# A graph network layer: node loads cut into rows of 2048 bytes and issued in one go, the first weight loads moved to GpSimd's queue

## The chip, the core and the metric

The kernel runs on one core of a Trainium2 chip. The metric is the device time of one execution in microseconds; the time of a kernel is the median of its runs. Five engines work side by side, each with its own queue of instructions: TensorE (PE in the profile; PEld is its weight load), VectorE (DVE), ScalarE (ACT), GpSimd (POOL) and SyncE (SP), which here only issues DMAs. DMAs are issued by SP, ACT and GpSimd; all of them are carried out by the same 16 DMA engines.

## What is computed

There are 12500 nodes with 160 features (64 scalars `s`, 32 vectors `v` of 3 components) and 400000 edges, sorted by destination.

```
h_s = s @ lin1_ws * a / sqrt(64)          # a: one number per node
h_v = v @ lin1_wv * a / sqrt(32)          # on the 32 channels, for each component
w   = silu(edge_attr_64 @ fc_w1 / 8) @ fc_w2 / 8        # 224 numbers per edge
es, ev = h_s[src], h_v[src]
messages per edge: w1*es*e0, w4*(ev . e1)/sqrt(3), (w2*es) e1, w3*ev*e0, w5*(ev x e1)/sqrt(2)
agg = sum of the messages over the edges of each destination / 4
o   = agg @ lin2, scaled by a; pre = x @ sc, scaled by a, + o
y   = silu of 64 scalars, sigmoid gates times the vectors
out = layernorm(x + y) over the 160 features
```

## The kernel before

**Three stages.** A first stage lays a table `h_tab` of `h_s` and `h_v` (12500 rows of 640 bytes) into device memory. The second stage walks over the 3125 tiles of 128 edges, in steps of four tiles: GpSimd gathers the table rows of each tile by its `src` indices (`gather`, L463, the indirect DMA of L467), TensorE makes the edge weights, VectorE the products, TensorE sums them into windows of 16 nodes, which are then mapped and added to the accumulator. The third stage, most of which lies inside the second, finishes blocks of nodes. A gather needs the whole table, so the second stage begins when the last row of `h_tab` has landed. A loop at the end, taken only for unusual destinations, does not run here.

**The first stage** (L226 to L360) works in six chunks of 2048 nodes (`CH`) and a last one of 212. For each chunk `load` issues three loads on SP: `xa` rows 0 to 63 (the scalars of x, transposed, L242), `xa` rows 64 to 127 (two components of the vectors, L243) and `xz` (the third component, in four quarters of 512 nodes, over 128 partitions, L248; L251 for the last chunk). TensorE multiplies 128 nodes at a time with `l1` (a block-diagonal matrix of lin1_ws and twice lin1_wv; L327) and with `l1z` (four times lin1_wv; L343); VectorE multiplies by the node attribute `at` into `ht` (L330, L346); GpSimd stores `ht` into `h_tab` (L357). Of `ht` there are three buffers, so chunk 3 reuses that of chunk 0 once its store has landed. Before chunk 3, `bases()` (L299) takes the first destination of each block of tiles from the first row of `dt` and spreads it over the partitions as `lo`. The last 84 rows of the table are stored by SP (L360).

**The order around the change.** All engines work in the order of the program text here (`manual_schedule`). SP issues the loads of chunk 0 first; ACT issues the loads of `at`, `l1` (three) and `l1z` (four), scales `l1` and `l1z` by 1/sqrt(64) or 1/sqrt(32) (L287) and issues the load of the first row of `dt` (L289). The node loads of the other chunks follow on SP, then the first indices and edge attributes (`ahead`, L152 and L153) and the edge network's weights (L296, L297). GpSimd makes the identity and three iotas before its first store. After the table GpSimd also issues the first edge features (`load_chunk(0, nc.gpsimd)`, L202) and the whole `dt` (L364), and then gathers for the rest of the kernel. The framework gives the DMAs of SP and ACT eight completion semaphores in rotation, those of GpSimd another eight; a DMA waits until the one that had its semaphore before has landed.

Of the kernel before, what the change touches and what calls it, by code (L numbers as in the profile page):

```python
# [10 lines left out]
F32 = mybir.dt.float32  # L11
# [9 lines left out]
P = 128  # L21
S = 64
V = 32
# [7 lines left out]
W = 16  # L31
Q = 4
KB = 4
# [20 lines left out]
def gnn_kernel(  # L54
# [21 lines left out]
    nc = tc.nc  # L76
    N = x.shape[0]
    NT = attr.shape[1]
# [4 lines left out]
    NB = -(-TT // BT)  # L83
    RATE = round(N / NB)
    assert NP >= N - 1 + W

    consts = ctx.enter_context(tc.tile_pool(name="consts", bufs=1))
# [71 lines left out]
    def index(t):  # L159
        a0, idx, _ = ahead(t)  # L160
        return idx[:, t - a0:t - a0 + 1]
# [32 lines left out]
    def load_chunk(c, queue=nc.sync, mark=None):  # L194
# [4 lines left out]
        for half, n in enumerate(halves):  # L199
# [4 lines left out]


    ident = consts.tile([P, P], F32, name="ident")
    make_identity(nc, ident)
    iota_i = consts.tile([P, W], I32, name="iota_i")
    nc.gpsimd.iota(iota_i, pattern=[[1, W]], base=0, channel_multiplier=0)
    eps = consts.tile([P, 1], F32, name="eps")  # L210
    nc.vector.memset(eps, 1e-5)

    w1 = consts.tile([2 * S, 2 * S], F32, name="w1")
    nc.vector.memset(w1, 0.0)

    w2 = consts.tile([2 * S, 2, NWT], F32, name="w2")
    nc.vector.memset(w2, 0.0)
    l2 = consts.tile([P, 11, V3], F32, name="l2")
    nc.vector.memset(l2, 0.0)
    share = ends_pool.tile([1, NB], I32, name="share")  # L220
    even = NB // (2 * KB) * 2 * KB
    nc.gpsimd.iota(share[:, :even], pattern=[[2 * KB * RATE, even // (2 * KB)], [RATE, KB], [KB * RATE, 2]],
                   base=0, channel_multiplier=0)
    nc.gpsimd.iota(share[:, even:], pattern=[[RATE, NB - even]], base=even * RATE, channel_multiplier=0)

    U = 4  # L226
    dt = ends_pool.tile([P, TT], I32, name="dt")
    lo = ends_pool.tile([P, NB], F32, name="lo")
    CH = 4 * U * P
    starts = list(range(0, N, CH))  # L230
    with tc.tile_pool(name="nodes", bufs=len(starts)) as nodes, tc.tile_pool(
        name="nodes_ps", bufs=6, space=PSUM
# [3 lines left out]
        def load(c0):  # L236

            cn = min(CH, N - c0)
            quarters = 4 if cn == CH else 1
            assert quarters == 4 or cn <= U * P  # L240
            xa = nodes.tile([P, CH], F32, name="xa")
            nc.sync.dma_start(xa[:S, :cn], xs_t[:, c0:c0 + cn])  # L242
            nc.sync.dma_start(xa[S:, :cn], xv_t[:2 * V, c0:c0 + cn])  # L243
            xz = nodes.tile([P, U * P], F32, name="xz")
            cq = cn // quarters
            z = xv_t[2 * V:, c0:c0 + cq]
            if quarters == 4:
                nc.sync.dma_start(xz[:, :cq], bass.AP(tensor=z.tensor, offset=z.offset,  # L248
                                                      ap=[[z.ap[0][0], V], [cq, 4], [1, cq]]))
            else:  # L250
                nc.sync.dma_start(xz[S:S + V, :cq], z)  # L251
            loaded.append((c0, cn, quarters, cq, xa, xz))

        load(starts[0])
        at = consts.tile([P, NT], F32, name="at")
        nc.scalar.dma_start(at, attr)

        l1 = consts.tile([P, P], F32, name="l1")
        nc.vector.memset(l1, 0.0)
        nc.scalar.dma_start(l1[:S, :S], lin1_ws)  # L260
        for i in range(2):
            r = slice(S + i * V, S + (i + 1) * V)
            nc.scalar.dma_start(l1[r, r], lin1_wv)
        scales = [(l1[:S], 1.0 / math.sqrt(S)), (l1[S:], 1.0 / math.sqrt(V))]

        def scale():
            for m, by in scales:
                nc.vector.tensor_scalar_mul(m, m, by)
            scales.clear()
# [8 lines left out]
                scales.append((m, scale))  # L278
            return m

        l1z = consts.tile([P, P], F32, name="l1z")
        nc.vector.memset(l1z, 0.0)
        for q in range(4):
            nc.scalar.dma_start(l1z[q:q + 4 * V - 3:4, q * V:(q + 1) * V], lin1_wv)
        scales.append((l1z, 1.0 / math.sqrt(V)))
        for m, by in scales:
            nc.scalar.mul(m, m, by)  # L287
        scales.clear()
        nc.scalar.dma_start(dt[0:1], dst[0:1])  # L289
        for c0 in starts[1:]:  # L290
            load(c0)
        index(0)
        raw = ends_pool.tile([2 * S, NWT], F32, name="raw")
        for half in range(2):
            r = slice(half * S, (half + 1) * S)
# [20 lines left out]
        for c0, cn, quarters, cq, xa, xz in loaded:  # L316
            if c0 == 3 * CH:
                bases()
            ht = nodes.tile([P, 4 * U, D], F32, name="ht", bufs=3)
            nt = -(-cn // P)  # L320
            first = c0 // P
            full = cn // P
            for t0 in range(0, nt, U):
                ps = nps.tile([P, U, P], F32, name="hp")
                for t in range(t0, min(t0 + U, nt)):
                    n = min(P, cn - t * P)
                    nc.tensor.matmul(ps[:n, t - t0], xa[:, t * P:t * P + n], l1,  # L327
                                     start=True, stop=True)
                k = min(U, full - t0)
                nc.vector.tensor_mul(  # L330
                    ht[:, t0:t0 + k, :P], ps[:, :k],
                    at[:, first + t0:first + t0 + k, None].to_broadcast([P, k, P]))
                if t0 + k < nt <= t0 + U:
                    n = cn - full * P
                    nc.vector.tensor_scalar(ht[:n, full, :P], ps[:n, full - t0],
                                            at[:n, first + full:first + full + 1], None, op0=OP.mult)

            pz = zps.tile([P, U, 4, V], F32, name="pz")
            r = slice(0, P) if quarters == 4 else slice(S, S + V)
            by = l1z if quarters == 4 else l1[r, r]  # L340
            for u in range(-(-cq // P)):
                n = min(P, cq - u * P)
                nc.tensor.matmul(pz[:n, u, :quarters].rearrange("p q c -> p (q c)"),  # L343
                                 xz[r, u * P:u * P + n], by, start=True, stop=True)
            if quarters == 4:
                nc.vector.tensor_mul(  # L346
                    ht[:, :, P:].rearrange("p (q u) c -> p u q c", q=4), pz,
                    at[:, first:first + 4 * U].rearrange("p (q u) -> p u q", q=4)[:, :, :, None]
                    .to_broadcast([P, U, 4, V]))
            else:  # L350
                nc.vector.tensor_mul(ht[:, :full, P:], pz[:, :full, 0],
                                     at[:, first:first + full, None].to_broadcast([P, full, V]))
            if cn > full * P:
                n = cn - full * P
                nc.vector.tensor_scalar(ht[:n, full, P:], pz[:n, full, 0],
                                        at[:n, first + full:first + full + 1], None, op0=OP.mult)
            nc.gpsimd.dma_start(  # L357
                h_tab[c0:c0 + full * P, :].rearrange("(q p) d -> p q d", p=P), ht[:, :full])
            if cn > full * P:
                nc.sync.dma_start(h_tab[c0 + full * P:c0 + cn, :], ht[:n, full])  # L360
# [6 lines left out]
    for half in range(2):  # L367
        r = slice(half * S, (half + 1) * S)
# [21 lines left out]
    for to, part, pieces, w, r0, c0, by in maps:  # L390
        for k, piece in enumerate(pieces):
# [3 lines left out]
            m = terms.setdefault((to, part, four), len(terms))  # L395
            at_r = at_p * V
            r = l2[at_r:at_r + V, m, c0:c0 + w.shape[1]]
# [270 lines left out]
    with tc.tile_pool(  # L668
        name="fin", bufs=1
    ) as fin, tc.tile_pool(  # L670
        name="late", bufs=2
    ) as late, tc.tile_pool(name="edge", bufs=2) as edge, tc.tile_pool(
        name="deep", bufs=4
# [164 lines left out]
        with tc.manual_schedule(engines={ENG.PE, ENG.DVE, ENG.Activation, ENG.Pool}):  # L838
# [46 lines left out]
            n = len(steps)  # L885
# [32 lines left out]
        with tc.For_i(0, n_redo, 1):  # L918
# [9 lines left out]
            with tc.For_i(0, n_again, 1) as g, tc.For_i(0, GT, 1) as k:  # L928
                t = g * GT + k
# [22 lines left out]
                r = edge.tile([P, 1], F32, name="r", bufs=1)  # L952
# [10 lines left out]
                with tc.For_i(first, last + 1, W) as base:  # L963
                    base = nc.s_assert_within(
                        base, 0, N - 1, skip_runtime_bounds_check_because="it is at most `last`")
# [61 lines left out]
```

## Time and profile before

| | before |
|---|---|
| median of 3 runs | 4039.55 us (4037.21 to 4057.42) |
| the profiled execution | 4041.38 us, its span 4039.6 us |
| busy: PE, DVE, ACT, POOL | 3650.5, 2437.3, 904.7, 3005.0 us |
| gathers (L467) | 3125, 957 ns each |
| first gather starts | 64.75 us |

The span is the time from the first to the last instruction; the little that the execution takes beyond it lies around it. The rows of the profile are read so: start and length in microseconds, the engine, the line of the kernel, the operation, what it writes and reads, how many; in brackets how long the engine had been idle and what ended that. "SPq" and the like are DMA issues. A row of waits says which engine and line waited for what, the sum, how often, and the longest.

### The profile page before, as it was taken

Reading aid. Unit: us, or ns where it says so; the run is one execution under the profiler, and the core shown is the slowest. Engines: PE = TensorE matmul, PEld = TensorE weight load, DVE = VectorE, ACT = ScalarE, POOL = GpSimd, SP = SyncE. Lnnn points to the kernel's source line nnn. Section 1 sums busy time; section 2 is a strip of 40 time slices with the busy share of each in tenths; the row PEclk is TensorE's granted clock in tenths of the full one; section 3 lists DMA queues with packets and bytes.
Section 4 is the critical chain, followed back from the end, with each engine's and each line's share of the span. In section 5 each row is a group of like instructions: output and inputs, shape, how many; then the busy total and the mean of one; then the engine's idle time right before and its main releaser. Section 6 shows DMA issues by size and latency. Waiting matters only on the chain.

```text
span 4039.6 us, 46290 instructions
## 1 busy us (share of the span) xinstructions
PE 3650.5 (90%) x14291; PEld 1592.7 (39%) x14291; DVE 2437.3 (60%) x6386; ACT 904.7 (22%) x2463; POOL 3005.0 (74%) x3144
## 2 busy tenths in 40 slices
PE   6898998989999989899899999898999999999897
PEld 4333343334334334333334343343344334334343
DVE  5655665655666656656656566565665655656656
ACT  2211221222222212212212122121221222222212
POOL 4777777777777777777777777777777777777775
PEclk8999999999999999999999999999999999999999
DMA  7433443444434434444444444444443444434432
GB/s 231 101 93 92 108 98 93 110 95 96 108 93 99 108 91 101 106 95 99 101 100 99 96 105 99 99 102 93 108 99 93 108 95 97 110 92 99 102 90 67
DMA packets 227689, 411.69 MB, mean 102 GB/s; under 512 B 71884, under 2 KB 157384, under 8 KB 226536
## 3 DMA queue, kind: packets, MB, share of 16 engines
q0 software_dynamic: 152272, 266.53, 27.7%
q1 hardware_dynamic: 74646, 142.01, 14.6%
q8 instruction: 115, 1.88, 0.2%
q14 instruction: 142, 1.16, 0.1%
q10 hardware_dynamic: 514, 0.10, 0.0%
HBM read 392.41 MB, written 16.00 MB: 101 GB/s over the span
## 4 chain that ended last, share of the span: by engine, by line
POOL 32%; issue 21%; PE 20%; DMA 13%; DVE 9%; DVEq 0%; ACT 0%; POOLq 0%; ACTq 0%
POOL hg L467 32%; DMA hg<-h_tab,idx 13%; PE pw L480 7%; PE pa L554 6%; DVE pr L498 5%; PE misc L583 3%; DVE pr L490 2%; PE misc L450 2%; PE misc L563 2%; DVE acc L591 1%; PE misc L617 0%; DVE oh L544 0%; DVE sel L547 0%; PE misc L732 0%; DVE st L641 0%
## 5 line engine op out<-in xcount | busy, mean ns | idle before, releaser
L467 POOL DMA_INDIRECT hg<-h_tab,idx x3125 | 2990.7, 957 | 961.9 <-issue 872.8
L480 PE MATMUL pw<-w,hid 128*128 128x448 f32 x3126 | 1390.9, 570 | 142.2 <-DVE pr L498 132.5
L490 DVE TENSOR_TENSOR pr<-pw,hg 128x512 f32<-128x512 f32 x782 | 540.0, 691 | 1452.9 <-DMA hg<-h_tab,idx 942.8
L554 PE MATMUL pa<-pr,sel 128*64 128x416 f32 x6250 | 1291.6, 535 | 0.0
L498 DVE TENSOR_TENSOR pr<-pw,hg 128x384 f32<-128x384 f32 x2346 | 1153.9, 547 | 0.0
L480 PEld LDWEIGHTS pw<-w,hid 128*128 128x128 f32 x3126 | 590.3, 198 | 707.2 <-issue 499.4
L554 PEld LDWEIGHTS pa<-pr,sel 128*64 128x64 f32 x6250 | 387.5, 139 | 874.8 <-issue 774.2
L566 ACT COPY tt<-misc 128x192 f32<-128x192 f32 x521 | 166.0, 319 | 2038.9 <-PE pw L480 2034.6
L450 PE MATMUL misc<-es,w 128*128 128x512 f32 (+1 forms) x784 | 416.7, 614 | 14.4 <-DMA scs<-in_sc_ws_dram 13.4
L547 DVE TENSOR_TENSOR sel<-oh,eas 128x256 f32<-128x256 f32 x782 | 338.2, 433 | 41.4 <-ACT eas L526 1.0
L563 PE MATMUL misc<-ident,sa 128*128 128x128 f32 x2084 | 345.4, 289 | 18.8 <-DVE acc L733 17.8
L563 PEld LDWEIGHTS misc<-ident,sa 128*128 128x128 f32 x2084 | 226.3, 143 | 322.4 <-issue 232.6
L583 PE MATMUL misc<-tt,l 128*96 128x256 f32 (+5 forms) x1496 | 347.4, 380 | 1.5 <-ACT tt L568 1.5
L454 ACT ACTIVATE hid<-misc 128x512 f32<-128x512 f32 x392 | 237.9, 607 | 399.6 <-PE pw L480 398.3
L766 ACT COPY sa<-pa 128x416 f32<-128x416 f32 x521 | 267.7, 514 | 235.1 <-PE pw L480 233.7
L583 PEld LDWEIGHTS misc<-tt,l 128*96 128x96 f32 (+1 forms) x1496 | 223.4, 162 | 128.0 <-issue 51.8
L591 DVE TENSOR_TENSOR acc<-acc,os 96x32 f32 x1042 | 193.8, 186 | 25.8 <-ACT os L586 6.4
L617 PE MATMUL misc<-ident,acc 96*128 96x96 f32 x196 | 40.5, 295 | 181.1 <-DVE acc L591 180.6
L544 DVE TENSOR_TENSOR oh<-rel,iota 128x64 f32<-128x64 int16 x782 | 169.9, 217 | 0.0
L450 PEld LDWEIGHTS misc<-es,w 128*128 128x128 f32 x784 | 118.6, 191 | 101.7 <-ACT sa L766 59.3
L586 ACT COPY os<-misc 96x512 f32<-96x512 f32 (+2 forms) x68 | 38.3, 563 | 371.4 <-PE misc L583 368.8
L617 PEld LDWEIGHTS misc<-ident,acc 96*128 96x128 f32 x196 | 21.6, 154 | 245.5 <-issue 160.1
(84 smaller groups left out, 717.1 us busy)
## 6 DMA issues: line engine op xcount, KB each, us to landing
es<-in_es_t_dram SPq DMA_DIRECT2D x258, 384.0 KB
hg<-h_tab,idx POOLq DMA_INDIRECT x3125
h_tab<-ht POOLq DMA_DIRECT2D x6, 1280.0 KB
xt<-in_x_dram SPq DMA_DIRECT2D x23, 320.0 KB
out_dram<-y SPq DMA_DIRECT2D x23, 320.0 KB
xv<-in_xv_t_dram SPq DMA_DIRECT2D x25, 187.5 KB
xs<-in_xs_t_dram SPq DMA_DIRECT2D x25, 125.0 KB
xa<-in_xs_t_dram SPq DMA_DIRECT2D x6, 512.0 KB
```

Of the source, the lines that this page charges most:

```text
L450: nc.tensor.matmul(ph[:k, c], w1[:k, :k], es[:k, t0 * P + c0 * P:t0 * P + c1 * P], start=True, stop=True)
L454: return nc.scalar.activation(hid[:k, c], ph[:k, c], AF.Silu, scale=1.0 / math.sqrt(64))
L467: nc.gpsimd.indirect_dma_start(out=hg[:, t, :], out_offset=None, in_=h_tab, in_offset=bass.IndirectOffsetOnAxis(ap=i, axis=0))
L480: last = nc.tensor.matmul(pw[:, t:t + m, :NWT], hid[:m * S, c * P:(c + 1) * P], w2[:m * S, :m], start=True, stop=True)
L490: nc.vector.tensor_mul(two, pw[:, :n, :2 * S].rearrange("p t (k c) -> p t k c", k=2), hg[:, :n, None, :S].to_broadcast([P, n, 2, S]))
L498: nc.vector.tensor_mul(pr[:, :n, first:first + V3].rearrange("p t (i c) -> p t i c", i=3), pw[:, :n, None, 2 * S + k * V:2 * S + (k + 1) * ...
L547: nc.vector.tensor_mul(sel[:, :n], oh[:, :, None, :].to_broadcast([P, n, 4, W]), by_slot(tiles[0][0])[:, u:u + n, :, None].to_broadcast([P ...
L554: return nc.tensor.matmul(pa[half * ROWS:(half + 1) * ROWS, :NPR], sel[:, t].rearrange("p k w -> p (k w)"), pr, start=start, stop=stop)
L563: nc.tensor.transpose(pt[:, four * P:four * P + k], sa[:k, c:c + P], ident[:k, :k])
L583: nc.tensor.matmul(po[:, k, :nb], l2[r, terms[to, part, four]], a[:, :nb], start=(n == 0), stop=(n == len(of) - 1))
L591: nc.vector.tensor_add(window, window, os[:, :, b])
L766: closed.append(lambda: nc.scalar.copy(sa, pa[:, :NPR]))
```

## The change

The order of the first stage is changed. The `memset`s of `eps`, `w1`, `w2` and `l2`, the identity and the iotas are put into a function `prepare()`, which is called later. `l1` and `l1z` are cleared first; then SP issues the node loads of all chunks one after the other. Each `xa` load of a full chunk is written as four quarters of 512 nodes, and `xa` has 8 more elements after each quarter, so that a partition's destination is four pieces of 2048 bytes and not one of 8192. The loads of `l1`, `at`, `l1z` and the first row of `dt` are issued by GpSimd instead of ACT, before `prepare()`. The scaling of `l1` and `l1z` is done by VectorE (`scale()`) and not by ACT. The arithmetic is the same.

```diff
     ident = consts.tile([P, P], F32, name="ident")
-    make_identity(nc, ident)
     iota_i = consts.tile([P, W], I32, name="iota_i")
-    nc.gpsimd.iota(iota_i, pattern=[[1, W]], base=0, channel_multiplier=0)
...
+    def prepare():
+
+        for m, by in ((eps, 1e-5), (w1, 0.0), (w2, 0.0), (l2, 0.0)):
+            nc.vector.memset(m, by)
+        make_identity(nc, ident)
+        nc.gpsimd.iota(iota_i, pattern=[[1, W]], base=0, channel_multiplier=0)
+        nc.gpsimd.iota(share[:, :even], pattern=[[2 * KB * RATE, even // (2 * KB)], [RATE, KB], [KB * RATE, 2]],
+                       base=0, channel_multiplier=0)
+        nc.gpsimd.iota(share[:, even:], pattern=[[RATE, NB - even]], base=even * RATE, channel_multiplier=0)
...
+    PAD = 8
...
-            xa = nodes.tile([P, CH], F32, name="xa")
-            nc.sync.dma_start(xa[:S, :cn], xs_t[:, c0:c0 + cn])
-            nc.sync.dma_start(xa[S:, :cn], xv_t[:2 * V, c0:c0 + cn])
+            xa = nodes.tile([P, 4, U * P + PAD], F32, name="xa")
+            for rows_of, w in ((slice(0, S), xs_t[:, c0:c0 + cn]), (slice(S, P), xv_t[:2 * V, c0:c0 + cn])):
+                if quarters == 4:
+                    nc.sync.dma_start(xa[rows_of, :, :U * P], w.rearrange("s (q c) -> s q c", q=4))
+                else:
+                    nc.sync.dma_start(xa[rows_of, 0, :cn], w)
...
-        load(starts[0])
-        at = consts.tile([P, NT], F32, name="at")
-        nc.scalar.dma_start(at, attr)
-
         l1 = consts.tile([P, P], F32, name="l1")
-        nc.vector.memset(l1, 0.0)
-        nc.scalar.dma_start(l1[:S, :S], lin1_ws)
+        l1z = consts.tile([P, P], F32, name="l1z")
+        for m in (l1, l1z):
+            nc.vector.memset(m, 0.0)
+        for c0 in starts:
+            load(c0)
+        nc.gpsimd.dma_start(l1[:S, :S], lin1_ws)
         for i in range(2):
             r = slice(S + i * V, S + (i + 1) * V)
-            nc.scalar.dma_start(l1[r, r], lin1_wv)
+            nc.gpsimd.dma_start(l1[r, r], lin1_wv)
+        at = consts.tile([P, NT], F32, name="at")
+        nc.gpsimd.dma_start(at, attr)
+        for q in range(4):
+            nc.gpsimd.dma_start(l1z[q:q + 4 * V - 3:4, q * V:(q + 1) * V], lin1_wv)
+        nc.gpsimd.dma_start(dt[0:1], dst[0:1])
+        prepare()
         scales = [(l1[:S], 1.0 / math.sqrt(S)), (l1[S:], 1.0 / math.sqrt(V))]
...
-        l1z = consts.tile([P, P], F32, name="l1z")
-        nc.vector.memset(l1z, 0.0)
-        for q in range(4):
-            nc.scalar.dma_start(l1z[q:q + 4 * V - 3:4, q * V:(q + 1) * V], lin1_wv)
         scales.append((l1z, 1.0 / math.sqrt(V)))
-        for m, by in scales:
-            nc.scalar.mul(m, m, by)
-        scales.clear()
-        nc.scalar.dma_start(dt[0:1], dst[0:1])
-        for c0 in starts[1:]:
-            load(c0)
+        scale()
         index(0)
...
-                    nc.tensor.matmul(ps[:n, t - t0], xa[:, t * P:t * P + n], l1,
+                    at_u = t % U * P
+                    nc.tensor.matmul(ps[:n, t - t0], xa[:, t // U, at_u:at_u + n], l1,
                                      start=True, stop=True)
```

## The prediction

> **What bounds the kernel now.** I read the waits of GpSimd first, then its instructions in order of time.
>
> ```profile
> POOL hg L467 <- issue: 872.8, 2865, 0.3
> POOL hg L467 <- DMA h_tab<-ht: 10.2, 1, 10.2
> ```
> ```profile
> 52.39 0.56 POOL L357 DMA_DIRECT2D h_tab<-ht  x1 [0.95 <-DVE ht L355]
> 52.94 1.09 POOL L202 DMA_DIRECT2D es<-in_es_t_dram  x2
> 54.00 0.59 POOL L364 DMA_DIRECT2D dt<-in_dst_dram  x1
> 64.75 1.04 POOL L467 DMA_INDIRECT hg<-h_tab,idx  x1 [10.16 <-DMA h_tab<-ht]
> ```
>
> GpSimd issues 3125 gathers. The first starts at 64.75 us, the last at 4006.19, so one starts every 3941.44 / 3124 = 1.262 us: 0.957 busy and 0.30 of issue. Only one wait of a gather is longer than 0.3 us, the first one's for the table, 10.2 us. So the end is set by three terms: the first gather (64.75), the stream (3941.4) and what follows the last gather (4039.6 - 4006.2 = 33.4). They are the span, 4039.6; 1.8 us lie around it, 4041.38 in all for the profiled execution, which stands 1.83 above the median of 4039.55. The change touches only what comes before the first gather. My question is therefore how far the 64.75 moves; a microsecond there is one of the total.
>
> What fills the 64.75 us? The windows (length, then each engine's busy time, granted clock, DMA share, GB/s), then SyncE's waits and issues:
>
> ```profile
> 2.00:6.00 4.00, 0.00 (x0) 0.00 (x0) 1.05 (x3) 0.00 (x0) 3.37 (x2) 1.00 1.08 241
> 6.00:10.00 4.00, 0.00 (x0) 0.00 (x0) 0.00 (x0) 1.85 (x3) 0.00 (x0) 1.00 0.34 48
> 10.00:23.40 13.40, 12.07 (x88) 11.75 (x89) 6.92 (x10) 0.36 (x2) 2.11 (x2) 1.00 1.03 244
> 34.00:44.80 10.80, 10.80 (x82) 10.80 (x83) 6.11 (x9) 0.32 (x2) 1.15 (x1) 0.83 1.03 374
> 52.40:59.90 7.50, 0.00 (x0) 0.00 (x0) 1.09 (x11) 0.00 (x0) 2.19 (x4) 0.65 1.04 331
> ```
> ```profile
> SPq L248 <- DMA l<-in_lin_ws_dram: 6.3, 1, 6.3
> ```
> ```profile
> 1.40 0.58 SPq L243 DMA_DIRECT2D xa<-in_xv_t_dram  x1
> 8.24 0.60 SPq L248 DMA_DIRECT2D xz<-in_xv_t_dram  x1
> ```
>
> The DMA engines are full from 10 us on, but between 6 and 10 us they move 48 GB/s. SyncE stands still from 1.98 to 8.24: SP's and ACT's DMAs get eight completion semaphores in rotation, and SP's third load got the one that ACT's lin1_ws load had. That load is itself late, behind the 8192-byte rows of the first chunk. This hole is what the change can close.
>
> **The change part by part.**
>
> *Loads in one go, small loads off ACT.* SP now issues 21 node loads with only its own semaphores, 0.6 us each (its rows), so eight are out by 0.76 + 8 x 0.6 = 5.6 us and the engines stay fed. The hole of 4 us would then carry 241 instead of 48 GB/s: 0.77 MB. At the 331 to 374 GB/s of the later windows that is 2.1 to 2.3 us of DMA time saved, at 244 GB/s 3.2.
>
> *When the compute starts.* Before, TensorE's first matmul (10.10) waits for ACT's scaling of l1 (9.74 + 0.31), which came after ACT's own blocked issues and a table load of 1.28. Now the first chunk's two xa loads (1.05 MB), from 2.0 us at 241 GB/s, are in at 6.4, landed at about 7. On GpSimd nine issues at 0.55 (es row: 1.09 for two) follow the l1 memsets at about 1.3: the third l1 load is out at 3.0, the last l1z at 5.7, dt at 6.3. From issue to landing I bound a small GpSimd DMA by the two gathers that the chain names in the first 200 us, 2.5 and 5.9: l1 is there at 5.5 to 8.9, l1z at 8.2 to 11.6. VectorE's three scalings cost 0.2 each (its 96x96 scaling at L268). So TensorE starts at 7.3 to 9.5, and VectorE's first multiplication, before at 12.21, needs l1z as well now and comes at 9.4 (2.1 of cold matmuls after 7.3) to 12.2. I take 9.5, since the rows here are light: a gain of 2.7 on the compute side. GpSimd's identity and iotas (0.2 + 0.3 + 0.15 + 3.9 + 0.12 = 4.7) move behind its issues and end at 11.0; the first table store goes out at 17.57 before and at about 14.9 after, so they stay hidden. Uncovered they would cost what is over 14.9, so nothing unless the nine issues take 4 us more. VectorE's memsets (1.6 together) end before l1 lands, else they add at most 1.6 to the scaling. The dt row is first needed in bases(), at 27.81 now. It lands by 12, at no cost.
>
> *Does this reach the gather?* Chunks 1 and 2 follow each other at 5.1 and 5.5 us now (17.57, 22.68, 28.19), partly load-bound: 1.31 MB at 244 GB/s is 5.4. So the shift stays about 2.7 to chunk 2. By 23.4, when the first store's packets start, 4.4 MB are loaded; after, by 20.7. From there chunks 3 to 5 meet the stores.
>
> *Rows of 2048 bytes.* They have two effects. First, beside the stores each engine takes packets of the two queues by turns, one for one: two windows of 2 us, the first with 2048-byte loads, the second mostly with 8192:
>
> ```profile
> q0 software_dynamic: 131, 0.59, 74.6%
> q1 hardware_dynamic: 125, 0.22, 29.3%
> ```
> ```profile
> q1 hardware_dynamic: 77, 0.50, 69.8%
> q0 software_dynamic: 75, 0.24, 39.2%
> ```
>
> Loads get 0.11 MB/us in small rows, 0.25 in large ones; the stores 0.30 and 0.12. The sum is 402 against 369 GB/s, so total work is no dearer. By the DMA records, packets of 2048 take 87 ns beside stores, those of 8192 355: the same bytes cost 348. Bounds of this term: 0 to 1.6 us lost (3072 rows, each 8.3 ns over a quarter of 315, which the fastest tenth of the 8192 rows take, on 16 engines); I take 0. Second, loads now lose against stores. From 20.7 the first three stores (3.93 MB at 0.30) last 13 us, if always at hand, while loads get 1.4 MB; the remaining 2.1 MB of chunks 3 to 5 run alone at 0.244, 8.6 us. Chunk 5 is then in at 42.3; before, its last load landed at 44.8. Store 3 doesn't come in between: it was issued at 41.35, 2.7 earlier is 38.6, and its packets began some 4 us after (first store: issue ended 18.96, packets 23.4). So the gain of 2.7 is not used up here.
>
> *The end of the stage.* The first gather waits for the last table rows, which SyncE stores (L360, issued at 52.47). By the landings the last GpSimd store is in at 59.84, SyncE's at 63.80: it stands behind its queue's small loads, each of which takes turns with a 4480-byte store packet. All of that begins when the node loads end, about 2.5 us earlier. Sum: -2.7 from the start, confirmed by -2.1 to -3.2 from the DMA work. First gather at 62.0; 4041.4 - 2.7 = 4038.7 profiled, median 4036.8.
>
> **Two rules of the skill.** 8192-byte rows alone take 565 ns (10 to 23.4 us) but 355 beside the stores, so the row is not the limit. The Trainium skill (SBUF — State Buffer, Door 1) says that partitions 0 to 63 reach only half of the DMA ports; by it the 2048-byte rows to the same halves load no faster alone, and the first 4.4 MB, which would take 11.8 us at 374 GB/s, keep the 18.0 that they take at 244. Against the change speaks the same page (section "SBUF: two separate sides", the warning on GpSimd's DMAs): DMAs issued by GpSimd wait while VectorE holds the shared port. Here gathers took 1.25 to 1.27 instead of 0.95 around 70 to 73 us, beside VectorE's 6.37 us of subtractions. [...]
>
> **The rivals.**
> *Given back (no change).* The tail store waits for other DMAs that are not earlier, and the engines are full anyway. For: DMA share 1.03 from 10 us on. Against: the hole is 3 us of pure idleness. 4039.6.
> *Slower: loads starved.* One mechanism: stores in 4480-byte packets take turns with 2048-byte rows, so if stores are at hand all the time, the 3.5 MB left at 20.7 need 32 us at 0.11 MB/us and end at 52.5 instead of 44.8. It decides once chunk 5 lands after 44.8. Half of that bound's 7.7 us, 3.9, gives 4043.4. Against: stores come only as fast as chunks are computed.
> *Tail freed.* If SyncE's small loads drain before the stores, the gather is released by GpSimd's last store, 59.84 - 2.7 + 0.95 = 58.1: -6.7, 4032.9.
> *Rows merged.* The descriptors may stay at 8192 bytes: the hole still closes, small loads land later (594 ns per row at the start), about -2: 4037.5.
>
> **How the numbers follow.** Forecast 0.50, given back 0.20, starved 0.12, tail freed 0.13, merged 0.05. Over 0.5% is 20.2 us, about what a measurement of this kernel can tell from no change. Up to 64 us 18.5 MB are moved (windows summed); at the best 2 us, 402 GB/s, that is 46 us, a saving of 18: the stage cannot give 20.2. Only the stream could, by 6.5 ns a gather, or a run like the third, 4057.42. Hence 0.04 faster, 0.94 same, 0.02 slower. The range reaches from the freed tail, less the 2.3 us between the two near runs (4037.21 and 4039.55), to the starved loads.
>
> **What would show it.** Right: SP's issues without a gap to 5.6 us, DMA over 200 GB/s from 2 to 10 us, first table store near 14.9, first gather near 62, gathers still every 1.262. Wrong: a first store after 17, chunk 5 landing after 45, packets of 8192 on SP's queue in the first 45 us, or a stream whose interval moves.

## The result and the profile after

The changed kernel takes 4070.62 us in the median of six runs (4067.26 to 4071.69), the kernel before 4045.26 (six runs, 4037.21 to 4057.42): a ratio of 1.006, 95% interval 1.0043 to 1.0077. It is slower by 25 us, where a gain of 2.7 was forecast. The profiled execution takes 4071.69 us, its span 4069.9, against 4041.38 and 4039.6.

The three terms of the prediction, read from the starts of the first and the last gather (us):

| | before | after | difference |
|---|---|---|---|
| first gather | 64.75 | 61.82 | -2.93 |
| first to last gather | 3941.44 | 3973.80 | +32.36 |
| last gather to the end | 33.4 | 34.3 | +0.9 |
| span | 4039.6 | 4069.9 | +30.3 |

So the stage that was changed gained what was forecast, and the stage that was not touched lost eleven times as much. First the instructions of the changed stage: GpSimd, SyncE and VectorE in order of time (start, length, what ended the idle time before).

```profile
1.49 0.71 POOL L263 DMA_DIRECT2D l<-in_lin_ws_dram  x1 [1.02 <-DVE w L218]
2.19 1.06 POOL L266 DMA_DIRECT2D l<-in_lin_wv_dram  x2
...
8.02 3.90 POOL L221 IOTA share<- 1x1040 int32 x1
...
19.57 1.25 POOL L358 DMA_DIRECT2D h_tab<-ht  x1 [7.53 <-DVE ht L347]
...
52.75 1.71 POOL L358 DMA_DIRECT2D h_tab<-ht  x2 [7.12 <-DVE ht L347]
...
61.82 1.04 POOL L468 DMA_INDIRECT hg<-h_tab,idx  x1 [5.69 <-issue]
```
```profile
0.76 0.76 SPq L244 DMA_DIRECT2D xa<-in_xs_t_dram  x1
...
4.95 0.62 SPq L244 DMA_DIRECT2D xa<-in_xs_t_dram  x1
5.62 0.62 SPq L244 DMA_DIRECT2D xa<-in_xv_t_dram  x1
```
```profile
6.65 0.22 DVE L277 TENSOR_SCALAR l<-l 64x128 f32<-64x128 f32 x1 [3.60 <-DMA l<-in_lin_ws_dram]
10.13 1.87 DVE L277 TENSOR_SCALAR l<-l 64x128 f32<-64x128 f32 x1 [3.26 <-DMA l<-in_lin_wv_dram]
12.90 0.23 DVE L277 TENSOR_SCALAR l1z<-l1z 128x128 f32<-128x128 f32 x1 [0.90 <-DMA l1z<-in_lin_wv_dram]
```

SyncE now issues without its stop of 6 us. But the small loads on GpSimd's queue land late, the scalings follow them, and the first table store goes out at 19.57, not at 14.9: 2.0 later than before. The first gather comes 2.9 earlier all the same. The windows (length, each engine's busy time, granted clock, DMA share, GB/s) show the closed hole:

```profile
2.00:6.00 4.00, 0.00 (x0) 0.00 (x0) 0.94 (x1) 0.04 (x1) 3.92 (x8) 1.00 0.95 198
6.00:10.00 4.00, 0.00 (x0) 0.00 (x0) 0.22 (x1) 0.00 (x0) 3.09 (x5) 1.00 1.07 219
10.00:23.40 13.40, 11.34 (x85) 11.35 (x86) 8.67 (x12) 0.00 (x0) 3.29 (x3) 1.00 1.07 222
```

From 6 to 10 us 219 GB/s move, not 48. But the windows before and after it move less than in the kernel before (198 against 241, 222 against 244 GB/s). Now the gathers: the group's row of the page of before and of after (busy time, mean ns of one, idle time before them), then the same instructions by minimum/median/maximum in ns.

```profile
L467 POOL DMA_INDIRECT hg<-h_tab,idx x3125 | 2990.7, 957 | 961.9 <-issue 872.8
```
```profile
L468 POOL DMA_INDIRECT hg<-h_tab,idx x3125 | 3022.6, 967 | 957.8 <-issue 873.4
```
```profile
L467 POOL DMA_INDIRECT hg<-h_tab,idx x3125: 942/946/1432, 64.7 to 4006.2; - x196
```
```profile
L468 POOL DMA_INDIRECT hg<-h_tab,idx x3125: 949/953/1799, 61.8 to 4035.6; - x196
```

The idle time before the gathers is the same. Each gather is longer: minimum and median by 7 ns, in each tenth of the execution. 3125 x 7 ns is 21.9 us of the 32.4. Gathers of 1000 ns and more make up most of the rest: 181 before, which exceed the median by 34.3 us in sum, and 210 after, by 44.0. The program line that gathers is unchanged; the semaphores that the gathers signal have other numbers (111 to 118 before, 101 to 108 after).

### The profile page after: what moved, and what is told of

Same layout as the page of the kernel before. It is cut to its first block, busy times and chain, and to the rows that moved or that the text cites. A ratio compares the mean times of both kernels' runs of the same rounds, so it can differ in the third digit from the quotient of the medians.

```text
span 4069.9 us, 46297 instructions
## 1 busy us (share of the span) xinstructions
PE 3650.2 (90%) x14291; PEld 1592.2 (39%) x14291; DVE 2437.5 (60%) x6389; ACT 903.7 (22%) x2460; POOL 3041.8 (75%) x3153
## 4 chain that ended last, share of the span: by engine, by line
POOL 32%; issue 22%; PE 17%; DMA 14%; DVE 11%; DVEq 0%; ACT 0%; POOLq 0%; ACTq 0%
POOL hg L468 32%; DMA hg<-h_tab,idx 14%; PE pw L481 6%; DVE pr L499 5%; PE pa L555 4%; DVE pr L491 3%; PE misc L584 3%; PE misc L451 2%; PE misc L564 2%; DVE acc L592 1%; DVE oh L545 1%; PE misc L618 0%; DVE sel L548 0%; DVE st L642 0%; PE misc L733 0%
## 5 line engine op out<-in xcount | busy, mean ns | idle before, releaser
L468 POOL DMA_INDIRECT hg<-h_tab,idx x3125 | 3022.6, 967 | 957.8 <-issue 873.4
```

Source lines behind the costliest of these rows:

```text
L468: nc.gpsimd.indirect_dma_start(out=hg[:, t, :], out_offset=None, in_=h_tab, in_offset=bass.IndirectOffsetOnAxis(ap=i, axis=0))
```

## The experiments

The question is what in a change of the first 60 us can make 3125 later gathers longer. The theories: **L**, the form or order of the node loads; **Q**, the number of DMAs on GpSimd's queue; **C**, any computation of GpSimd after a DMA of its own; **O**, the order of GpSimd's first instructions: a DMA ahead of its first computations. Against O stands **N** in the last runs: the longer gather is a mark of the changed stage or is hidden, and costs no time by itself.

On some chips TensorE was granted a clock of about 0.88 instead of 0.96, gathers then start every 1.59 us, and times there are compared only with the kernel before on the same chip; the length of a gather can be read on either. All results in one table, in order of the median gather. "DMA ahead" says whether GpSimd issues a DMA ahead of its first iota.

| run | DMA ahead | gather min/median, ns | first gather, us | time, us | ratio to before on its chip |
|---|---|---|---|---|---|
| before | no | 942/946 | 64.75 | 4041.38 | |
| e1 | no | 942/946 | 65.58 | 4045.01 | |
| e2 | no | 942/946 | 63.59 | 4054.70 | 1.001 (1.0001 to 1.0020) |
| e7 | no | 940/946 | 64.10 | 5099.37 | |
| e9 | no | 942/946 | 68.53 | 4066.18 | 1.0001 (0.9992 to 1.0011) |
| e10 | no | 942/946 | 63.05 | 4057.27 | |
| e12 | no | 942/946 | 70.50 | 4084.85 | |
| e3 | no | 942/947 | 65.94 | 4051.77 | 1.000 (0.999 to 1.0009) |
| e11 | no | 942/949 | 68.40 | 4074.79 | |
| e15 (as e2) | no | 942/949 | 63.29 | 5103.50 | 1.000 (0.998 to 1.0021) |
| after | yes | 949/953 | 61.82 | 4071.69 | 1.006 (1.0043 to 1.0077) |
| e18 (as after) | yes | 949/953 | 61.19 | 4074.68 | 1.0067 (1.0053 to 1.0080) |
| e17 | yes | 949/953 | 62.78 | 4073.03 | 1.0067 (1.0053 to 1.0081) |
| e13 (as after) | yes | 947/953 | 63.13 | 5077.85 | 0.9951 (0.9934 to 0.9968) |
| e16 | yes | 947/953 | 66.19 | 5091.81 | |
| e5 | yes | 947/953 | 62.97 | 5079.32 | 0.9927 (0.990 to 0.9953) |
| e4 | yes | 949/954 | 62.31 | 4088.65 | |
| e6 | yes | 947/956 | 65.78 | 5068.66 | |
| e8 | yes | 947/956 | 62.83 | 5061.56 | |
| e14 (as e17) | yes | 950/957 | 64.96 | 5075.06 | 0.9955 (0.9934 to 0.9977) |

A time with a ratio is a median, one without is that of the profiled execution.

**e1, the kernel before once more; e2, the nine small loads back on ACT's queue.** e2 keeps the rows of 2048 bytes, the loads in one go and VectorE's scaling.

```diff
-        nc.gpsimd.dma_start(l1[:S, :S], lin1_ws)
+        nc.scalar.dma_start(l1[:S, :S], lin1_ws)
...
-        nc.gpsimd.dma_start(dt[0:1], dst[0:1])
+        nc.scalar.dma_start(dt[0:1], dst[0:1])
```

> The kernel before, once more with a profile, to see whether its gathers (median 946 ns, one every 1.262 us on average) are the same in another execution. Every theory that puts the difference into the program expects 946 again. A theory by which the length of a gather is drawn anew in each execution expects any value, 953 (as after the change) among them.

> The changed kernel with the nine small loads (l1, at, l1z, first row of dt) back on ACT's queue; node loads in one go, 2048-byte rows and VectorE's scaling stay. Theory Q (nine early DMAs on GpSimd's queue make each later gather 7 ns longer): gathers at 946 ns median, interval 1.262, first gather 60 to 65, total 4036 to 4046. Theory L (the node loads' form or order does it): gathers stay at 953, total about 4068 to 4072.

e1 gives 946 again, so the length belongs to the program. e2 gives 946 too, with all node loads in their new form: theory L is out. Its time is 4 us above the kernel before, at the edge of what the runs tell apart.

**e3, prepare() ahead of the nine loads; e4, a tenth small load.**

```diff
+        prepare()
         nc.gpsimd.dma_start(l1[:S, :S], lin1_ws)
...
-        prepare()
```
```diff
         nc.gpsimd.dma_start(dt[0:1], dst[0:1])
+        nc.gpsimd.dma_start(dt[1:2], dst[1:2])
```

> The changed kernel with prepare() (identity and iotas on GpSimd, memsets on VectorE) ahead of GpSimd's nine loads, so GpSimd computes before it issues its first DMA, as in the kernel before. Theory O (it is the order of GpSimd's first instructions: a DMA issued before its first affine select and iotas): gathers at 946 ns, first gather 4 to 5 us later than after the change (66 to 67), total 4040 to 4050. Theory Q (the number of DMAs on its queue, wherever they stand): gathers stay at 953, total 4070 to 4076.

> The changed kernel with a tenth small load on GpSimd's queue (the second row of dt, which the later load of the whole dt writes again). Theory Q in its sharper form (the place in the queue's ring that the first DMAs leave): the gathers' median moves to another value, up or down by several ns. Theory O, or any theory in which only the kind of the first instruction counts: 953 again, total within 3 us of 4070.

e3 has all that the change has; identity and iotas only come first. Its gathers take 942/947, and the loss is gone (ratio 1.000):

```profile
L468 POOL DMA_INDIRECT hg<-h_tab,idx x3125: 942/947/2327, 65.9 to 4014.1; - x196
```

So the nine DMAs on GpSimd's queue cost the stream nothing by themselves. In e4 the tenth load moves the median by 1 ns; the 4088.65 of this run comes for the most part from 290 gathers of 1000 ns and more, which exceed the median by 56.9 us in sum (44.0 in after).

**e5, the identity ahead of the loads, the iotas behind; e6, the kernel before with one load, the first row of dt, as GpSimd's first instruction; e7, the kernel before with the nine loads on GpSimd's queue, behind identity and iotas; e8, after with four loads ahead of prepare() and five behind.**

```diff
-        make_identity(nc, ident)
...
+        make_identity(nc, ident)
         nc.gpsimd.dma_start(l1[:S, :S], lin1_ws)
```
```diff
+    dt = ends_pool.tile([P, TT], I32, name="dt")
+    nc.gpsimd.dma_start(dt[0:1], dst[0:1])
     ident = consts.tile([P, P], F32, name="ident")
...
-    dt = ends_pool.tile([P, TT], I32, name="dt")
...
-        nc.scalar.dma_start(dt[0:1], dst[0:1])
```
```diff
-        nc.scalar.dma_start(at, attr)
+        nc.gpsimd.dma_start(at, attr)
...
-        nc.scalar.dma_start(dt[0:1], dst[0:1])
+        nc.gpsimd.dma_start(dt[0:1], dst[0:1])
```
```diff
         nc.gpsimd.dma_start(at, attr)
+        prepare()
...
         nc.gpsimd.dma_start(dt[0:1], dst[0:1])
-        prepare()
```

> The changed kernel with only the identity (a memset and the affine select on GpSimd) ahead of the nine loads; the three iotas stay behind them. Theory O (what counts is that a DMA is issued before GpSimd's first real compute instruction): gathers at 946 to 947 ns, first gather 62 to 63, total 4040 to 4048, so below the kernel before. Theory I (all of GpSimd's compute has to stand first): gathers still above 949, total over 4055.

> The kernel before with one load alone, the first row of dt, on GpSimd's queue as its first instruction, ahead of identity and iotas; everything else as before. Theory O: gathers at 953 as after the change, total 4066 to 4075. Theory Q (it is the number of DMAs ahead): one of nine, so 946 to 947, total within the spread of the kernel before.

> The kernel before with all nine small loads on GpSimd's queue, behind its identity and iotas; node loads, rows and ACT's scaling as before. Theory O: 946 to 947 ns, as with prepare() first. Theory Q: 953. The first gather moves by a few us at most.

> The changed kernel with four of the nine loads (l1 and at) ahead of prepare() and five (l1z, first row of dt) behind it. Theory O: 953 as after the change, since a DMA still comes first. A dose theory (each DMA ahead of the compute adds its part): a median between 947 and 953.

These four met a chip with the low clock, so their times do not answer the question; the gathers do. One load ahead is enough (e6, 956), nine behind do nothing (e7, 946): Q is out. The identity first does not help (e5, 953). Theory O had expected 946 there, so if it holds, the iotas and not the identity are the computations that count. The dose theory expected a median between 947 and 953 in e8; it is 956, as in e6 with one load.

**e9, the kernel before with iota_i behind the first table store; e10, with a memset of GpSimd behind the last table store; e11, after with the iotas first and the identity behind the nine loads; e12, the kernel before with all of GpSimd's DMAs but the gathers on ACT's queue.**

```diff
-    nc.gpsimd.iota(iota_i, pattern=[[1, W]], base=0, channel_multiplier=0)
...
+            if c0 == 0:
+                nc.gpsimd.iota(iota_i, pattern=[[1, W]], base=0, channel_multiplier=0)
```
```diff
+    late_zero = consts.tile([P, 1], F32, name="late_zero")
+    nc.gpsimd.memset(late_zero, 0.0)
     load_chunk(0, nc.gpsimd)
```
```diff
-        nc.gpsimd.iota(iota_i, pattern=[[1, W]], base=0, channel_multiplier=0)
...
+        nc.gpsimd.iota(iota_i, pattern=[[1, W]], base=0, channel_multiplier=0)
...
+        nc.gpsimd.iota(share[:, even:], pattern=[[RATE, NB - even]], base=even * RATE, channel_multiplier=0)
         nc.gpsimd.dma_start(l1[:S, :S], lin1_ws)
```
```diff
-            nc.gpsimd.dma_start(
+            nc.scalar.dma_start(
...
-    load_chunk(0, nc.gpsimd)
-    nc.gpsimd.dma_start(dt, dst)
+    load_chunk(0, nc.scalar)
+    nc.scalar.dma_start(dt, dst)
```

> The kernel before with one instruction moved: GpSimd's small iota (iota_i, 128 x 16, 0.15 us) stands behind its first table store and no longer ahead of it. No load changes its queue. Theory C (a compute instruction of GpSimd that follows a DMA on its queue leaves every later DMA there some 7 ns longer, however many DMAs there are): gathers at 953 to 957 ns, first gather within 1 us of 65, stream longer by some 22 to 32 us where GpSimd bounds it, total 1.005 to 1.008 of the kernel before. Theory E (it takes a DMA ahead of the first compute instruction, early in the program): 946, ratio 1.000.

> The kernel before with one more instruction: a memset of one number per partition on GpSimd, behind its last table store and ahead of the first edge features' load. Theory C with any kind of compute: gathers at 953 to 957 ns. [...]

> The changed kernel with the three iotas ahead of the nine loads and the identity (memset and affine select) behind them, the other half of the test with the identity first. Theory C: 953 to 957 ns, since an affine select follows the DMAs. A theory by which the iotas alone do it: 946 to 949.

> The kernel before with the table stores, the first edge features and the whole dt on ACT's queue instead of GpSimd's, so that the gathers are the only DMAs that GpSimd issues, behind its identity and iotas. Theory C: 946 ns, nothing computes after a DMA. A theory by which the plain DMAs ahead of the gathers cost them time, many or few: below 946. The first gather moves by some us either way with the stores' queue.

A memset or an iota that comes after a DMA leaves the gathers at 946 (e9, e10), as long as another iota has come before it: C is out. Without any other DMA on GpSimd's queue a gather is no shorter than before (e12). On the chip of these runs the kernel before itself took 4066.48, and its variants had 256 to 354 gathers of 1000 ns and more. That number moves with the chip, which is why only the minimum and the median are read here.

**e13 to e16, on one chip with the low clock: after, e6, e2 again, and the kernel before with the dt load between identity and iotas. e17 and e18, on a chip with the usual clock: e6 and after again.** The edit of e16 is that of e6 with the load behind `make_identity`.

> The changed kernel once more, on one chip beside the next three. Theory O (a DMA that GpSimd issues ahead of its first affine select and iotas lengthens every later gather; the shift of 7 ns and not the order of the loads is the change's loss): median gather 953 again, against 946 of the kernel before; the stream 22 us longer by the shift, 10 us or less by more of the long gathers, first gather 3 us earlier: 20 to 30 us slower than the kernel before, ratio 1.005 to 1.0075. Rival (chance: the first result was drawn from a bad pair of runs, the gathers' 7 ns are made up for by shorter gaps elsewhere): within 10 us of it.

> The kernel before with nothing changed but one load of 320 bytes or so, the first row of dt, which GpSimd issues as its very first instruction and not ACT. Theory O: median gather 953 to 957, the time 22 to 34 us above the kernel before, ratio 1.0055 to 1.0085, though the table comes no later. Rival N (the longer gather is a mark of the changed kernel's whole first stage, or is hidden behind TensorE where the clock is low, and costs no time by itself): the time within 10 us of the kernel before.

> The changed kernel with its nine small loads on ACT's queue again (node rows of 2048 bytes, loads in one go and VectorE's scaling kept), beside the two above on one chip. Theory O: gather 946, time within 5 us of the kernel before, 20 us or more below the changed kernel. Rival L (the node loads' form costs the stream): like the changed kernel.

> The kernel before with the load of the first row of dt on GpSimd's queue between the identity and the three iotas. If what counts is that any DMA comes ahead of the last of GpSimd's first computations: gather 949 to 957. If it has to come ahead of the affine select of the identity: 946 to 947.

> The kernel before with the first row of dt loaded by GpSimd as its first instruction, once more. Where GpSimd's stream of gathers sets the interval (about 1.26 us a tile): theory O gives 22 to 34 us over the kernel before, ratio 1.0055 to 1.0085; rival N a time within 10 us of it. Where TensorE's low clock sets the interval (about 1.59 us a tile): like the run before this, ratio 0.993 to 0.998 by both, and the question stays open.

> The changed kernel beside the one-load kernel on the same chip. Theory O: gather 953; where the gathers set the interval, 15 to 35 us over the kernel before (ratio 1.004 to 1.009) and within 10 us of the one-load kernel less the 3 us of its earlier table. Rival N: 10 us or more above the one-load kernel. Where TensorE sets the interval: ratio 0.993 to 0.998.

e16 splits GpSimd's first computations. Its instructions in order of time, and those of e17, which has the same load two places earlier:

```profile
1.03 0.29 POOL masks.py:199 TENSOR_SCALAR_AFFINE_SELECT ident<-ident 128x128 f32<-128x128 f32 x1
1.52 0.73 POOL L209 DMA_DIRECT2D dt<-in_dst_dram  x1 [0.20 <-issue]
2.25 0.19 POOL L211 IOTA iota_i<- 128x16 int32 x1
```
```profile
1.32 0.71 POOL L207 DMA_DIRECT2D dt<-in_dst_dram  x1 [0.86 <-POOLq L1015]
2.02 0.25 POOL masks.py:197 MEMSET ident<- 128x128 f32 x1
```

And their gathers by minimum/median/maximum in ns, e16 first:

```profile
L467 POOL DMA_INDIRECT hg<-h_tab,idx x3125: 947/953/1813, 66.2 to 5048.3; - x196
```
```profile
L467 POOL DMA_INDIRECT hg<-h_tab,idx x3125: 949/953/1553, 62.8 to 4033.4; - x196
```

Both have the longer gathers. Semaphores are not the cause: those of e16's gathers are 110 to 117, as in e2 and e15, and those of e5's 105 to 112, as in e3 and e7. In every run of the table with a DMA ahead of the first iota the shortest gather takes 947 to 950 ns, in every run without one 940 to 942. The two groups do not touch. Order and time are not told apart by these runs: with "yes" the first DMA of GpSimd starts at 1.3 to 1.5 us, with "no" at 4.9 us (e11) or later, since the 3.90 us iota comes first. A DMA ahead of the iota and a DMA in the first few microseconds are the same thing here. The median is less sharp: it differs by 3 to 4 ns between chips for one program (946 and 949 for e2 and e15, 953 and 957 for e17 and e14).

e17 settles the price. It differs from the kernel before in one small load, and on the chip where the gathers set the interval it costs what the whole change costs: 4073.03 and 4074.68 against 4047.42, the same ratio of 1.0067. By its profile the stream from first to last gather is 3970.6 us, 29.1 more than the 3941.4 of the kernel before in the first section; the 7 ns make 21.9 of these. Rival N, that the longer gather costs no time, is out.

On the chip with the low clock the sign is the other one: after 0.9951, e14 0.9955, e15 1.000. The 20 us and more that theory O expected above the kernel before did not come in e13 and e14. There GpSimd waits some 1000 us in all for a free buffer; on the usual clock the same row reads 14.0 us in after. Of e15's and of e13's waits of GpSimd, these:

```profile
POOL hg L468 <- DVE oh L545: 1050.3, 286, 7.1
```
```profile
POOL hg L468 <- DVE oh L545: 1005.3, 278, 7.1
```

The chain that ended last runs over PE for 43% and 45% of the span, over GpSimd for 1%; in e13:

```profile
PE 45%; another core or an unknown queue 33%; issue 8%; ACT 6%; DVE 5%; POOL 1%; DMA 1%; DVEq 0%; ACTq 0%; POOLq 0%
```

So 7 ns more in a gather can be hidden there. What does set the interval on that chip is not shown: TensorE is busy for 77% of the span in e13 and 78% in e15, and for a third of the chain the profile names no releaser. That the early DMA even makes these runs 0.5% faster goes together with a somewhat higher granted clock: TensorE is busy for 3925.8 us at 0.889 in e13 and for 3952.7 at 0.882 in e15, the same product within 0.2%. Why a longer gather should raise the clock is open.

No version beats both kernels: e3 and e2, which keep the loads in one go, stand at 1.000 and 1.001.

## Why the prediction failed

**The stream.** The step that failed is the sentence "The change touches only what comes before the first gather". It was taken as given that 1.262 us per gather hold whatever comes first. Nine DMAs were moved past the identity and the iotas on GpSimd's queue, and this order was priced by what it delays ("so they stay hidden"). Shown: with the DMA first, each gather takes 6 to 7 ns more (947 in e3 against 953 in after, 946 in before against 953 in e17), and the time is 1.0067 of the kernel before in e17, 1.000 in e3. Why it does so stays open. The prediction itself worked out what would be needed for 20 us, "6.5 ns a gather", and gave it 0.02 on the slow side; the row of before offered no reason for it, but no bound either. The remaining 10 us of the stream are the longer gathers of 1000 ns and more. Their number was 216 and 219 in e17 and e18, near after's 210, but with the chip's own spread (181 and 187 in two profiles of the kernel before, 174 in e3) it is not shown that they belong to the order.

**When the compute starts: wrong.** l1 was expected at 5.5 to 8.9, TensorE at 7.3 to 9.5, the first store at 14.9. Measured: 10.13 for the load, 12.05 for TensorE, 19.57 for the store. Two terms were mis-sized. A small load of GpSimd, beside SyncE's node loads, took up to 7 us from its issue (l1's second and third: issued by 3.25, landed by 10.1); the bounds came from gathers of the first 200 us, 2.5 and 5.9. And the second scaling took 1.87 us and not 0.2. It ends at 12.00, 0.1 us after the 3.90 us iota (8.02 to 11.92), which the prediction had put there and called hidden. In e3, where the iotas are over by 5.4, the same instruction takes 0.23; VectorE's rows of that kernel:

```profile
13.26 0.22 DVE L277 TENSOR_SCALAR l<-l 64x128 f32<-64x128 f32 x1 [10.21 <-DMA l<-in_lin_ws_dram]
14.21 0.23 DVE L277 TENSOR_SCALAR l<-l 64x128 f32<-64x128 f32 x1 [0.73 <-DMA l<-in_lin_wv_dram]
```

So the iota had a waiter that no semaphore shows. The Trainium skill (SBUF — State Buffer, section "Who interferes with whom") names it: a tensor_scalar may enter the mode that needs the port pair shared with GpSimd, and who starts first keeps the pair for the whole instruction. Trace and page agree, with 1.65 us as the price here. In e8, whose iota runs from 4.49 to 8.39, it is the first scaling that takes 2.01 us and ends at 8.47. The direction that the prediction had weighed, GpSimd's DMAs held up by VectorE, did not show: GpSimd's two issues at 2.19, beside VectorE's memset of 0.94 us, took 0.53 each as elsewhere.

**The first gather: right in size, not by its way.** 62.0 was forecast, 61.82, 61.19 and 63.13 were measured for the changed kernel. But the compute started 2 us later, not 2.7 earlier. That the gather does not follow the compute is seen best in e7: its first store goes out at 24.48, 6.9 later than before, its first gather starts at 64.10.

The closed hole did not bring the gain either, so the 2.1 to 3.2 us of DMA time saved, which the prediction took as confirmation, were not there in the end. The lead that the hole gives is used up early: by the DMA records 6.7 MB have moved by 30 us in both kernels, and by 50 us 13.9 MB, before 14.0. The node loads end later and not 2.5 earlier: chunk 5's last load lands at 46.04, before at 44.77.

What came earlier is the end of the stage. In the profile of after, SyncE's table store lands at 56.53, before at 63.80. GpSimd's last store lands at 60.78, before at 59.84, and the gather starts 1.04 after it. By the DMA records SyncE's queue has 425 packets between 54 and 56 us, where GpSimd's queue takes 63% of the engines; before it had 76, beside 92%. This is the rival "tail freed", at less than half of its 6.7 us, because GpSimd's last store came 0.94 later and not 2.7 earlier. "Starved" came in part too: chunk 5's store is issued at 52.75, before at 50.28, and the last store follows it on the same queue. That the outcome met the forecast 2.7 is luck. In e13 SyncE's store is again the last to land, at 62.18, and the gather starts at 63.13. Of the prediction's signs of being wrong, three came: a first store after 17 us, chunk 5 landing after 45, and an interval that moves (1.262 to 1.272 us).

**Rows of 2048 bytes.** The 10 to 23.4 us window moves 222 GB/s, before 244. Rows of 2048 bytes loaded no faster than those of 8192; this agrees with the Trainium skill's rule on the ports of partitions 0 to 63 (SBUF — State Buffer, Door 1). The term was taken as 0, and here it was a loss: by the DMA records 155 ns for a row of 2048 bytes in this window, against 565 for one of 8192 before, which is 141 for the same bytes.

## What to carry to other kernels

A long stream of equal instructions multiplies any constant: before calling it untouched, ask what a nanosecond in each is worth, and compare its minimum and median between two profiles, not only its mean. On GpSimd, put the iotas ahead of its first DMA when the rest of the kernel is a stream of its gathers that sets the time; one DMA moved past them gave the whole loss here (e17), and putting them back was the whole cure (e3). And an instruction moved "into a gap" can hold another engine without a semaphore: look at the lengths of its neighbours, not only at who waits for it.

## What the runs showed of the hardware

*The order at the start stays visible to the end.* A DMA issued by GpSimd ahead of its first iota makes each later indirect DMA of 128 rows longer: 947 to 950 ns at least instead of 940 to 942, to the last gather 4 ms later. One load is enough, nine or ten add no more than 1 ns, and the identity ahead of it changes nothing. Node loads, number and semaphores of the DMAs, and later computations do not do it. All these early DMAs start by 1.5 us and none of the others before 4.9, so it may be the early time and not the order that counts. In e9 the long iota stayed ahead of the DMAs, so the first iota and the long one are not told apart. What it leaves behind in GpSimd, and why a DMA ahead of it matters, was not found.

*Long gathers meet VectorE's work.* Of the 181 gathers of 1000 ns and more in the kernel before, 155 overlap the product L547 (sel from oh and eas, both in SBUF); of the other gathers 23% do. In after it is 183 of 210 against 22%. The sum L591 is also met more often: by 104 of the 181, and by 15% of the others. This is an association and was not tested by an experiment.

*The same edit can have two signs.* Where the chip grants TensorE 0.96 the early load costs 0.67%, where it grants 0.88 the kernel is 0.5% faster with it, for a reason that was not found. A difference of this size must name the clock under which it was measured.
